# A graph layer's node update moved into the edge loop's buffers, with its inputs asked for in the last six groups and the last groups summed as small batches

## The chip, the cores and the metric

One core of one Trainium2 chip runs the kernel as one launch. The metric is the device time of that launch in microseconds (us); lower is better. The kernel before takes 4115.59 us (median of 3 runs, 4114.87 to 4116.8).

A core has five engines with a queue of instructions each: TensorE (PE; its weight loads are shown apart as PEld), VectorE (DVE), ScalarE (ACT), GpSimd (POOL) and SyncE (SP). [...] DMA transfers are started from a queue (SP's, ACT's or POOL's) and land later.

## The reference

A graph of 12,500 nodes with 64 features and 412,500 edges with 32 features, the edges sorted by receiver. Cut to what matters:

```python
h = relu(layernorm(x))
msg_in = concat(h[senders], h[receivers], edge)          # 412,500 x 160
messages = silu(msg_in @ W1 + b1) @ W2 + b2
logits = silu(msg_in @ Wa1 + ba1) @ Wa2 + ba2
att = softmax(logits, axis=0)                            # over all edges
agg = segment_sum(messages * att, receivers)             # per node
x = x + silu(concat(h, agg) @ Wu1 + bu1) @ Wu2 + bu2     # the node update
```

The softmax runs over all edges of the graph, so its maximum and its sum are known only at the end. The kernel keeps a running maximum and corrects what was summed under an older one.

## The kernel before, in words

**Head.** Nodes are normalised and two tables are written to DRAM: `ts_d` (sender's half of the first layer) and `tr_d` (receiver's half).

**Edge loop.** 403 groups (NG) of 1,024 edges each, as 8 tiles of 128 (K = 8). Each group `g` goes through these steps, which are functions in `one_pass`:

- `load(g)`: POOL starts eight indirect gathers of sender rows into a `gs` tile (L487; a ring of 8 `gs` tiles). Every eleventh group takes one of the eight tiles with row loads from SP in its place. SP loads the receivers' windows (`wins`, L506, three in turn) and, every fourth group, edge features `eo` and receivers' numbers `db` for four groups (two buffers of each in pool `work2`). DVE builds a selection in `eo` (L513), and PE multiplies it with the windows into the PSUM tile `pe` (L517; three tiles `pe` of two banks each).
- `begin(g)`: DVE adds `pe` and `gs` (L523), ACT takes the tanh (L526).
- `end(g)`: DVE makes the message (L536, kept in one of eight `acts` tiles) and the logits (L542, L544, L547). When `g` closes a batch, `top` reduces the batch's logits and transposes the maximum on PE (L557 to L564).
- `weigh(s)`: DVE takes the running maximum `nmax` from it (L571 to L574), ACT makes the factor `scale` for older sums (L575) and the weights `p` (L578). A new batch starts every 4 groups, and `starts` ends with the single groups 400, 401 and 402.
- `sum_up(g)`, which runs five groups late: `by_node` (DVE makes weighted selections, L588; PE sums edges to nodes into `sp`, L594), `out_of` (ACT copies `sp`, L600), `project` (PE, L605) and `put` (DVE adds the result to `sums` and notes the maximum in `stand`, L618 to L624). `put` works for one group two steps after its `by_node`.

`pin` keeps the order of the program among the instructions that it wraps; DMA starts are not pinned, and a scheduler places them in SP's queue. The PSUM tile `mt` exists once and is shared by the projection and the transposed maximum.

In groups 399 to 402 the loop drains: `upto` says how many further `sum_up` calls follow each `end`, and all of them are over when the loop ends.

**Node update** (L715 to L790). Thirteen tiles of 8 x 128 nodes, the last one of 2 x 128. Pools of its own are opened after the loop: `upd` in SBUF (three buffers of each name) and `upd_ps` in PSUM (`fac` twice, `th` twice, `po` three times). Per tile `t`:

- `sums_of`: SP loads `bu_in` from `bq_d` (L741) and `xb` from `xb_d` (L743), 256 KB each. Both were computed during the edge loop. ACT makes the correction `fac` = exp (L746), DVE scales `sums` with it and with the softmax's inverse (L750), POOL adds `bu_in` (L755).
- `silu`: ACT's tanh `th` (L759), then DVE (L760).
- `second`: four matmuls on PE into `po` (L767; the profile counts each fp32 matmul twice).
- `rest`: DVE adds `xb` (L773), SP writes two halves to the output (L775).

The loop over tiles is skewed:

```python
for t in range(NT + 2):
    if t < NT:
        sums_of(t)
    if 1 <= t <= NT:
        silu(t - 1)
        second(t - 1)
    if t >= 2:
        rest(t - 2)
```

Of the kernel before, what the change touches and what calls it, by code (L numbers as in the profile page):

```python
# [45 lines left out]
I32 = mybir.dt.int32  # L46
# [318 lines left out]
def one_pass(tc, n_edges, v):  # L365
# [11 lines left out]
    starts = list(range(0, NG - 3, B)) + [NG - 3, NG - 2, NG - 1]  # L377
# [5 lines left out]
    with ExitStack() as ctx:  # L383
# [7 lines left out]
        base_hi = keep.tile([1, NG + 1], I32, name="base_hi")  # L391
        nc.vector.tensor_scalar(base_lo[:, :NG], base_sb[:, :NG], float(NH), float(W),
# [10 lines left out]
        nc.vector.memset(start[:, 1:2], BIG)  # L403
        w2u = keep.tile([S1, 2, U], F32, name="w2u")
# [9 lines left out]
        with tc.tile_pool(name="work2", bufs=2) as work2, \  # L414
# [57 lines left out]
            def registers(g, engine, at, base=base_sb, top=NP - 1):  # L472
                n = min(NQ, NG - g)
                _, regs = nc.values_load_multi_w_load_instructions(
                    base[0:1, g:g + n], engines=[engine], min_val=0, max_val=top,
                    skip_runtime_bounds_check_because=WHY)
                for i in range(n):
                    at[g + i] = regs[i]

            def load(g):  # L480

                t = g * K
                if g % NQ == 0:
                    registers(g, ENG.SP, at_sp)
                gs = gss[g] = gather.tile([P, K, C], F32, name="gs")
                for j in range(K - (g in alone)):
                    nc.gpsimd.indirect_dma_start(  # L487
                        out=gs[:, j, :], out_offset=None, in_=ts_d[:, :],
                        in_offset=bass.IndirectOffsetOnAxis(ap=src_sb[:, t + j:t + j + 1], axis=0))
                if g % NQ == 0:  # L490
                    n = min(NQ, NG - g) * E2
                    eo = work2.tile([P, NQ, E2], F32, name="eo")
                    db = work2.tile([WR, NQ, E2], I32, name="db")
                    for i in range(g, min(g + NQ, NG)):
                        ees[i] = eo[:, i - g, :], db[:, i - g, :]
                    nc.sync.dma_start(eo.rearrange("p g e -> p (g e)")[WR:, :n],
                                      edge[:, g * E2:g * E2 + n])
                    for r in range(2):
                        nc.sync.dma_start(
                            db.rearrange("p g e -> p (g e)")[r * R:(r + 1) * R, :n],  # L500
                            bass.AP(tensor=dst_row.tensor, offset=dst_row[r:r + 1, g * E2:].offset,
                                    ap=[[0, R], [1, n]]))
                eo, db = ees.pop(g)
                win = wins[g % WINS]
                for r in range(2):
                    nc.sync.dma_start(win[r * R:(r + 1) * R, :, r, :],  # L506
                                      tr_w[bass.ds(at_sp[g], R), :, :])
                for q in range(len(QUEUES)):
                    if QUEUES[q][0] == ENG.SP:
                        rows(q, g)  # L510
                for h in range(2):
                    e = slice(h * E2 // 2, (h + 1) * E2 // 2)
                    pin(nc.vector.tensor_scalar(eo[:WR, e], db[:, e], bj[:, g, h:h + 1], None,  # L513
                                                op0=ALU.is_equal))
                pe = pes[g] = pre_ps.tile([P, K, C], F32, name="pe")
                for q in range(H):
                    pin(nc.tensor.matmul(pe[:, 2 * q:2 * q + 2, :], eo[:, q * P:(q + 1) * P],  # L517
                                         win[:, q // 2, :, :], start=True, stop=True))
# [9 lines left out]
            def end(g):  # L528
# [18 lines left out]
                pin(nc.vector.tensor_reduce(lgs[s][:, k:k + K], att, AX.X, ALU.add))  # L547
                if g == starts[s] + size[s] - 1:
                    mts[s] = top(s)
# [58 lines left out]
            def put(g):  # L608

                if g % NQ == 0:  # L610
# [3 lines left out]
                pp = pps.pop(g)  # L614
                for h, at in enumerate((at_lo, at_hi)):
                    rows, cols = slice(h * U, (h + 1) * U), bass.ds(at[g], W)
                    if g == starts[s]:
                        pin(nc.vector.scalar_tensor_tensor(sums[rows, cols], sums[rows, cols],  # L618
                                                           scale[rows, s:s + 1], pp[rows],
                                                           op0=ALU.mult, op1=ALU.add))  # L620
                    else:
                        pin(nc.vector.tensor_tensor(sums[rows, cols], sums[rows, cols], pp[rows],  # L622
                                                    ALU.add))
                    pin(nc.vector.tensor_copy(stand[rows, cols],  # L624
                                              nmax[rows, s + 1:s + 2].to_broadcast([U, W])))
# [4 lines left out]
            def weigh_upto(s):  # L630
                while weighed[0] <= s:
                    weigh(weighed[0])
                    weighed[0] += 1

            def sum_up(g):
# [11 lines left out]
                if g is not None:  # L647
                    s = batch[g]
                    weigh_upto(s)
                    if g == starts[s]:  # L650
                        pin(nc.vector.scalar_tensor_tensor(total, total, scale[:, s:s + 1],
                                                           psums.pop(s), op0=ALU.mult, op1=ALU.add))
# [7 lines left out]
            for g in range(NG):  # L660
                more = None
                if done <= g - B - 1 or g >= NG - 3 and done < g:
# [16 lines left out]
                if more:  # L679
                    next(more)  # L680
                end(g)
# [3 lines left out]
                if g >= NG - 4:  # L685
                    upto = g + (-3, -1, 0, 1)[g - NG + 4]
                    for i in list(range(done, upto)) + [None, None] * (g == NG - 1):
                        for _ in sum_up(i):
                            pass
                        if i == done and g < NG - 1:  # L690
                            weigh_upto(batch[g])
                    done = max(done, upto)
# [22 lines left out]

        with tc.tile_pool(name="upd1", bufs=1) as upd1, \
                tc.tile_pool(name="upd", bufs=3) as work, \
                tc.tile_pool(name="upd_ps", bufs=2, space=PSUM) as upd_ps:
            sv, fv = (t[:, W:W + NH].rearrange("f (p b) -> f p b", b=NB) for t in (sums, stand))
            last = nmax[:, NS:NS + 1]  # L720
            ones = upd1.tile([P, P], F32, name="ones")
            nc.vector.memset(ones, 1.0)
            all_ps = upd_ps.tile([P, P], F32, name="all_ps", bufs=1)
            nc.tensor.matmul(all_ps[:, 0:1], ones, total, start=True, stop=True)
            inv = upd1.tile([P, 1], F32, name="inv")
            nc.vector.reciprocal(inv, all_ps[:, 0:1])

            tc.mark_branch_hint_location("again", "LikelyTaken",
                                         engines=[ENG.SP, ENG.DVE, ENG.PE, ENG.Activation])
            assert NB % 2 == 0  # L730
            bs, xs, us, ths, pos = {}, {}, {}, {}, {}

            def width(t):
                return min(NC, NB - t * NC)

            def sums_of(t):

                n = width(t)
                cols = P // 2 * n
                bs[t] = work.tile([P, P // 2 * NC], F32, name="bu_in")[:, :cols]  # L740
                nc.sync.dma_start(bs[t], bq_d[t, :, :cols])  # L741
                xs[t] = work.tile([P, NC * D], F32, name="xb")[:, :n * D]
                nc.sync.dma_start(xs[t], xb_d[t, :, :n * D])  # L743
                at = slice(t * NC, t * NC + n)
                fac = upd_ps.tile([P, P // 2 * NC], F32, name="fac")[:, :cols]
                pin(nc.scalar.activation(fac.rearrange("u (p b) -> u p b", b=n), fv[:, :, at], AF.Exp,  # L746
                                         bias=last, scale=-1.0))
                us[t] = work.tile([P, P // 2 * NC], F32, name="uT")[:, :cols]
                for k in range(2):
                    pin(nc.vector.scalar_tensor_tensor(  # L750
                        us[t].rearrange("u (k p i) -> u k p i", k=2, i=n // 2)[:, k],
# [3 lines left out]
                pin(nc.gpsimd.tensor_tensor(us[t], us[t], bs.pop(t), ALU.add))  # L755

            def silu(t):
                th = upd_ps.tile([P, P // 2 * NC], F32, name="th")[:, :P // 2 * width(t)]
                pin(nc.scalar.activation(th, us[t], AF.Tanh, scale=0.5))  # L759
                pin(nc.vector.scalar_tensor_tensor(us[t], th, 1.0, us[t], op0=ALU.add, op1=ALU.mult))  # L760

            def second(t):
                n = width(t) // 2
                uv = us.pop(t).rearrange("u (m i) -> u i m", i=n)
                po = pos[t] = upd_ps.tile([P, H, 2, D], F32, name="po", bufs=3)[:, :n]
# [3 lines left out]
            def rest(t):  # L769
                n = width(t)  # L770
                res = work.tile([P, NC * D], F32, name="res")[:, :n * D]
# [6 lines left out]

            for t in range(NT + 2):
                if t < NT:  # L780
                    sums_of(t)
# [7 lines left out]
            for _ in range(3):  # L789
                pin(nc.vector.memset(work.tile([P, NC * D], F32, name="res")[:, 0:1], 0.0))  # L790
# [246 lines left out]
```

## Time and profile before

| what | value |
|---|---|
| median of 3 runs | 4115.59 us |
| the profiled execution's own time / its span | 4115.52 us / 4113.8 us |
| POOL busy (gathers almost alone) | 3035.8 us, 74% |
| DVE busy | 3021.4 us, 73% |
| PE busy / PEld busy | 2284.8 us / 1852.9 us |
| ACT busy | 584.3 us, 14% |
| last gather starts | 4042.24 us |
| DVE begins the last group (`begin(402)`) | 4050.81 us |
| DVE begins the node update (first L750) | 4066.28 us |
| last output's DVE step begins | 4107.0 us |
| DMA rate, 4066.3 to 4110 us | 216 GB/s |

A row of a timeline gives start, busy time, engine, line, operation, tiles, shape and count; in brackets stands how long the engine was idle before it, and what ended that. SPq is the time in which SP starts DMAs. A window's row gives the busy time of each engine in a stretch, with the clock that TensorE was granted, the busy share of the DMA engines and what they moved. The page's part on the chain that ended last is empty for this run, so the end is followed by hand in the timeline.

### The profile page before, as it was taken

What the parts mean: (1) busy time and instruction counts of PE and PEld (TensorE: products, weight loads), DVE (VectorE), ACT (ScalarE), POOL (GpSimd) and SP (SyncE); (2) the same over time, 40 slices, a digit from 0 to 9 for tenths busy, and PEclk for the clock granted to TensorE, in tenths of its full rate; (3) what the DMA queues carried; (4) which work ended last, traced back from release to release, by engine and by line L of the source; (5) the groups of instructions that cost most, each with busy time, mean ns of one, the idle gap of its engine ahead of it and who ended that gap; (6) DMA issues with size and microseconds to landing.
All of it is one profiled execution on the core that took longest, in us unless ns stands there. A gap on an engine that the chain in (4) does not pass through costs nothing.

```text
span 4113.8 us, 59789 instructions
## 1 busy us (share of the span) xinstructions
PE 2284.8 (56%) x10980; PEld 1852.9 (45%) x10980; DVE 3021.4 (73%) x8518; ACT 584.3 (14%) x1235; POOL 3035.8 (74%) x3213
## 2 busy tenths in 40 slices
PE   5555545555556555556555555555555555555555
PEld 4444434444445444444444444444444444444444
DVE  6777867777777777777777777777777777777777
ACT  3211111111111111111111111111111111111112
POOL 3777777777777777777777777777777777777773
PEclk8666666666565666665566666666666556566665
DMA  7344443443434333333333333333333333333334
GB/s 270 88 102 101 99 105 92 105 101 97 102 93 99 86 91 84 88 91 81 91 84 89 91 81 91 83 89 91 81 91 82 91 91 81 92 81 90 91 78 112
DMA packets 220602, 393.50 MB, mean 96 GB/s; under 512 B 77077, under 2 KB 146554, under 8 KB 207034
## 3 DMA queue, kind: packets, MB, share of 16 engines
q0 software_dynamic: 102016, 209.13, 20.8%
q1 hardware_dynamic: 116826, 170.81, 17.0%
q10 hardware_dynamic: 1376, 9.67, 0.6%
q14 instruction: 294, 2.41, 0.2%
q8 instruction: 90, 1.47, 0.2%
HBM read 363.58 MB, written 25.72 MB: 95 GB/s over the span
## 4 chain that ended last, share of the span: by engine, by line


## 5 line engine op out<-in xcount | busy, mean ns | idle before, releaser
L487 POOL DMA_INDIRECT gs<-ts_d,src_sb x3188 | 3018.7, 947 | 1022.1 <-issue 952.1
L517 PE MATMUL pe<-wins,eo 128*128 128x256 f32 x3224 | 1477.3, 638 | 967.7 <-DVE eo L513 819.6
L517 PEld LDWEIGHTS pe<-wins,eo 128*128 128x128 f32 x3224 | 1000.5, 325 | 1265.8 <-DVE eo L513 970.2
L523 DVE TENSOR_TENSOR gs<-pe,gs 128x1024 f32<-128x1024 f32 (+1 forms) x403 | 487.7, 1211 | 775.5 <-DMA gs<-ts_d,src_sb 740.0
L526 ACT ACTIVATE pe<-gs 128x1024 f32<-128x1024 f32 x403 | 413.8, 1027 | 2585.7 <-DVE gs L523 1997.7
L588 DVE TENSOR_SCALAR wt<-iota_w,dloc,p 128x40 f32<-128x40 f32 x3224 | 734.0, 320 | 0.1
L594 PE MATMUL sp<-wt,acts 128*65 128x40 f32 x6448 | 608.9, 267 | 0.7 <-DVE wt L588 0.7
L594 PEld LDWEIGHTS sp<-wt,acts 128*65 128x65 f32 x6448 | 578.7, 183 | 1.0 <-DVE wt L588 0.8
L605 PEld LDWEIGHTS mt<-ss,w2u 65*128 65x128 f32 x806 | 224.8, 293 | 371.3 <-issue 321.5
L513 DVE TENSOR_SCALAR eo<-db,bj 64x256 f32<-64x256 int32 x806 | 259.7, 360 | 158.6 <-DMA db<-in_dst_row_dram 151.5
L564 PE MATMUL mt<-ident,mx 128*128 128x128 f32 x103 | 45.1, 437 | 547.3 <-DVE sums L622 538.2
L605 PE MATMUL mt<-ss,w2u 65*128 65x40 f32 x806 | 184.9, 324 | 261.4 <-DVE gm L571 257.9
L542 DVE SCALAR_TENSOR_TENSOR pe<-pe,gs 128x512 f32<-128x512 f32 x403 | 281.3, 698 | 13.0
L544 DVE TENSOR_TENSOR pe<-pe,w_all 128x512 f32<-128x512 f32 x403 | 281.4, 698 | 12.8
L536 DVE SCALAR_TENSOR_TENSOR acts<-pe,gs 128x512 f32<-128x512 f32 x403 | 278.2, 690 | 15.7 <-ACT pe L526 4.0
L547 DVE TENSOR_REDUCE lg<-pe 128x8 f32<-128x512 f32 x403 | 278.4, 691 | 13.7
L564 PEld LDWEIGHTS mt<-ident,mx 128*128 128x128 f32 x103 | 18.4, 179 | 557.7 <-issue 556.0
L624 DVE COPY stand<-nmax 64x40 f32 x806 | 163.4, 203 | 0.6
L622 DVE TENSOR_TENSOR sums<-sums,mt 64x40 f32 x600 | 113.2, 189 | 15.0 <-PE mt L605 10.9
L575 ACT ACTIVATE scale<-fall 128x1 f32<-128x1 f32 x103 | 20.9, 203 | 645.1 <-DVE fall L574 629.2
L600 ACT COPY ss<-sp 65x40 f32<-65x40 f32 x403 | 73.5, 182 | 20.7 <-PE sp L594 20.3
L618 DVE SCALAR_TENSOR_TENSOR sums<-sums,scale,mt 64x40 f32 x206 | 51.6, 251 | 11.4 <-PE mt L605 7.3
(92 smaller groups left out, 577.7 us busy)
## 6 DMA issues: line engine op xcount, KB each, us to landing
one_gs<-ts_d SPq DMA_DIRECT2D x4608, 0.5 KB
eo<-in_edge_dram SPq DMA_DIRECT2D x100, 512.0 KB
db<-in_dst_row_dram SPq DMA_DIRECT2D x200, 256.0 KB
gs<-ts_d,src_sb POOLq DMA_INDIRECT x3188
wins<-tr_d SPq DMA_DIRECT2D x806, 32.0 KB
ts_d<-ts SPq DMA_DIRECT2D x5, 896.0 KB
tr_d<-tr ACTq DMA_DIRECT2D x5, 896.0 KB
hT_d<-hT ACTq DMA_DIRECT2D x1, 3136.0 KB
```

The lines of the kernel that those rows point to most:

```text
L487: nc.gpsimd.indirect_dma_start(out=gs[:, j, :], out_offset=None, in_=ts_d[:, :], in_offset=bass.IndirectOffsetOnAxis(ap=src_sb[:, t + j:t ...
L513: pin(nc.vector.tensor_scalar(eo[:WR, e], db[:, e], bj[:, g, h:h + 1], None, op0=ALU.is_equal))
L517: pin(nc.tensor.matmul(pe[:, 2 * q:2 * q + 2, :], eo[:, q * P:(q + 1) * P], win[:, q // 2, :, :], start=True, stop=True))
L523: pin(nc.vector.tensor_tensor(gss[g][:, :n, :], pes[g][:, :n, :], gss[g][:, :n, :], ALU.add))
L526: pin(nc.scalar.activation(pes[g], gss[g], AF.Tanh))
L536: pin(nc.vector.scalar_tensor_tensor(acts[g % ACTS][:, :, 0:U], th[:, :, U:C], 1.0, gs[:, :, U:C], op0=ALU.add, op1=ALU.mult))
L542: pin(nc.vector.scalar_tensor_tensor(att, th[:, :, 0:U], 1.0, gs[:, :, 0:U], op0=ALU.add, op1=ALU.mult))
L544: pin(nc.vector.tensor_tensor(att, att, wa2[:, None, :].to_broadcast([P, K, U]), ALU.mult))
L547: pin(nc.vector.tensor_reduce(lgs[s][:, k:k + K], att, AX.X, ALU.add))
L588: pin(nc.vector.tensor_scalar(wt[:, j, :], iota_w[:, j // H, :], dloc[:, g * K + j:g * K + j + 1], p[:, k + j:k + j + 1], op0=ALU.is_equal ...
L594: pin(nc.tensor.matmul(sp, acts[g % ACTS][:, j, :], wt[:, j, :], start=j == 0, stop=j == K - 1))
L605: pin(nc.tensor.matmul(pp, w2u.rearrange("s h u -> s (h u)"), sps.pop(g), start=True, stop=True))
```

## The change

Three things change; all of them lie in the last six groups, the node update, and set-up ahead of the loop.

- **Batches.** The last starts are 392, 396, 398, 399, 400, 401, 402: two batches more (105 in place of 103). The extra `sum_up` calls are made after groups 396 to 399, one each, and from group 397 on each group also has one of its own. Groups 400 and 401 have one each, and group 402's steps are written out by hand behind the loop.
- **Inputs.** `bu_in` and `xb` of all 13 tiles are loaded by `inputs(t)`, called after groups 398, 399 and 401, into `eo` and `db` buffers (tiles 0 to 7) and into five `gs` tiles (8 to 12). `eo` and `db` are moved for it from `work2` to two fixed buffers of each.
- **Update in the loop's buffers.** `ut` and `res` are the two halves of three `gs` tiles. `fac`, `th` and `po` share three `pe` tiles: `fac` and `th` in the first bank of a tile, `po` in the second. `fac` of tile t + 1 is now made before `th` of tile t - 1.

The rest of the diff: `base_lo` and `base_hi` are zeroed, `ones` and `inv` move to set-up, and the branch hint moves ahead of the last group. In `put`, the parts `sums` and `stand` can be called apart.

```diff
-    starts = list(range(0, NG - 3, B)) + [NG - 3, NG - 2, NG - 1]
+    starts = list(range(0, NG - 7, B)) + [NG - 7] + list(range(NG - 5, NG))
...
+        nc.vector.memset(base_lo, 0)
+        nc.vector.memset(base_hi, 0)
...
+        eos = [keep.tile([P, NQ, E2], F32, name=f"eo{i}") for i in range(2)]
+        dbs = [keep.tile([P, NQ, E2], F32, name=f"db{i}") for i in range(2)]
...
-                    eo = work2.tile([P, NQ, E2], F32, name="eo")
-                    db = work2.tile([WR, NQ, E2], I32, name="db")
+                    eo = eos[g // NQ % 2]
+                    db = dbs[g // NQ % 2][:WR].bitcast(I32)
...
+            def inputs(t):
+                n = P // 2 * NC
+                if t < 8:
+                    i = (t // 4 + (NG - 1) // NQ + 1) % 2
+                    bs[t], xs[t] = (b[i][:, t % 4, :n] for b in (eos, dbs))
+                else:
+                    gs = gather.tile([P, K, C], F32, name="gs").rearrange("p k c -> p (k c)")
+                    bs[t], xs[t] = gs[:, :n], gs[:, n:]
+                m = width(t)
+                bs[t], xs[t] = bs[t][:, :P // 2 * m], xs[t][:, :m * D]
+                nc.sync.dma_start(bs[t], bq_d[t, :, :P // 2 * m])
+                nc.sync.dma_start(xs[t], xb_d[t, :, :m * D])
...
-                if done <= g - B - 1 or g >= NG - 3 and done < g:
+                if done <= g - B - 1 or g >= NG - 6 and done < g:
                     more, done = sum_up(done), done + 1
...
-                if g >= NG - 4:
-                    upto = g + (-3, -1, 0, 1)[g - NG + 4]
-                    for i in list(range(done, upto)) + [None, None] * (g == NG - 1):
-                        for _ in sum_up(i):
-                            pass
-                        if i == done and g < NG - 1:
-                            weigh_upto(batch[g])
-                    done = max(done, upto)
+                if NG - 7 <= g < NG - 3:
+                    for _ in sum_up(done):
+                        pass
+                    done += 1
+                    if g == starts[batch[g]] + size[batch[g]] - 1:
+                        weigh_upto(batch[g])
+                for t in {NG - 5: [0, 1], NG - 4: [2, 3], NG - 2: range(4, NT)}.get(g, []):
+                    inputs(t)
...
+            two, one = at[1], at[0]
+            end(NG - 1, then=lambda: put(two))
+            out_of(one)
+            weigh_upto(NS - 1)
+            totals(NS - 1)
+            project(one)
+            by_node(NG - 1)
+            put(one, "stand")
+            put(NG - 1, "stand")
+            put(one, "sums")
+            last = nmax[:, NS:NS + 1]
+            free = [gather.tile([P, K, C], F32, name="gs").rearrange("p k c -> p (k c)") for _ in range(3)]
+            uts, outs = ([f[:, i * P // 2 * NC:(i + 1) * P // 2 * NC] for f in free] for i in range(2))
+            free_ps = [pre_ps.tile([P, K, C], F32, name="pe") for _ in range(3)]
...
+            def factor(t):
+                n = width(t)
+                fac = facs[t] = free_ps[t % 3].rearrange("p k c -> p (k c)")[:, :P // 2 * n]
...
             def silu(t):
+                n = P // 2 * width(t)
+                ut, th = uts[t % 3][:, :n], free_ps[t % 3].rearrange("p k c -> p (k c)")[:, :n]
...
             def second(t):
+                po = pos[t] = free_ps[t % 3][:, H:, :].rearrange("p i (h d) -> p i h d", h=2)[:, :n]
...
+            factor(0)
+            all_ps = one_ps.tile([P, 4, P], F32, name="mt")[:, 0, :]
+            pin(nc.tensor.matmul(all_ps[:, 0:1], ones, total, start=True, stop=True))
+            pin(nc.vector.reciprocal(inv, all_ps[:, 0:1]))
+            out_of(NG - 1)
+            project(NG - 1)
+            put(NG - 1, "sums")
             for t in range(NT + 2):
                 if t < NT:
-                    sums_of(t)
+                    first(t)
+                if t + 1 < NT:
+                    factor(t + 1)
                 if 1 <= t <= NT:
                     silu(t - 1)
                     second(t - 1)
```

`first(t)` is the DVE and POOL part of the old `sums_of`.

## The prediction, made before the changed kernel had run

> **What bounds the kernel now.** I read the page's totals first, then windows over the last 130 us, then the timeline there, then its waits.
>
> ```profile
> L487 POOL DMA_INDIRECT gs<-ts_d,src_sb x3188 | 3018.7, 947 | 1022.1 <-issue 952.1
> ```
>
> 947 ns of gather and 0.30 us of issue make 1.25 us; 3188 of them make 3977 us, the whole way from about 66 us to the last gather. POOL paces the loop at 9.98 us per group (8 gathers). A DVE group has 7.9 us of work (below), so nothing before group 396 sets the end, and the change leaves POOL's gathers alone. Only what follows the last gather counts, some 71 us.
>
> ```profile
> 4015.00:4026.00 11.00, 5.38 (x29) 4.41 (x29) 10.53 (x35) 1.33 (x3) 8.27 (x9) 0.66 0.23 55
> 4026.00:4040.00 14.00, 9.90 (x67) 8.77 (x67) 12.54 (x49) 2.51 (x10) 10.64 (x12) 0.62 0.21 52
> 4040.00:4051.00 11.00, 5.33 (x41) 4.80 (x40) 10.38 (x38) 1.70 (x6) 2.57 (x3) 0.50 0.13 25
> 4051.00:4066.30 15.30, 8.40 (x57) 7.37 (x56) 11.64 (x49) 3.34 (x11) 0.00 (x0) 0.50 0.06 12
> 4066.30:4082.00 15.70, 11.29 (x43) 10.30 (x43) 12.71 (x26) 7.43 (x13) 7.59 (x6) 0.59 0.80 249
> 4082.00:4107.30 25.30, 14.90 (x57) 13.35 (x56) 13.14 (x27) 6.55 (x12) 8.00 (x7) 0.58 0.72 209
> ```
>
> Columns: PE, PEld, DVE, ACT, POOL busy, TensorE clock, DMA share, GB/s. From group 399 (4015) DVE is full: 10.53 of 11.00, 12.54 of 14.00, 10.38 of 11.00. In the update it is full until 4082 (12.71 of 15.70) and then half idle (13.14 of 25.30), with DMA at 72 to 80%.
>
> ```profile
> 4042.24 0.94 POOL L487 DMA_INDIRECT gs<-ts_d,src_sb  x1 [0.30 <-issue]
> ...
> 4050.81 1.22 DVE L523 TENSOR_TENSOR gs<-pe,gs 128x1024 f32<-128x1024 f32 x1 [0.21 <-issue]
> ...
> 4066.28 1.66 DVE L750 SCALAR_TENSOR_TENSOR uT<-sums,inv,fac 128x256 f32<-128x256 f32 x4
> ```
>
> A group's DVE start follows its last gather's start by 2.83 us when it waits for it (gather at 4012.28, DVE at 4015.11). The last group could begin at 4045.07; it begins at 4050.81, because DVE is behind by 5.7 us. From there to the first L750 are 15.5 us, and from L750 to the span's end 47.5 us.
>
> ```profile
> POOL uT L755 <- DMA bu_in<-bq_d: 13.8, 5, 5.0
> ```
>
> In the update POOL waits 13.8 us for `bu_in` (plus part of a first wait). Undisturbed, L773 follows itself by 2.2 us (4072.53 to 4081.29 for four tiles), which is DVE's own work of 2.24 us per tile (0.86 + 0.69 + 0.69).
>
> **What a page says.** The Trainium skill, "PSUM — Partial Sum Buffer", sections Terms and Specifications, forbids two engines on one bank and quadrant at once, and lets engines work side by side in different banks. By that rule `fac`/`th` in one bank of a `pe` tile and `po` in the other need no wait on each other. The trace of before cannot show the case: there `fac`, `th` and `po` are tiles of their own, and `fac` follows `th` without a wait (4086.13, 4086.67 below). I go by the changed program as built. In it `fac` of tile t + 3 waits for the last matmul of tile t, the very count that L773's successor (`rest` of tile t) waits for. The two share a tile, and the program makes one wait for the other though their banks differ.
> For the loads beside the gathers, "DMA: Bandwidth & Descriptors", Queues, rings and completion order, says each DMA engine takes turns among the queues it has work for. So loads share with the gathers rather than block them; before, 55 GB/s run in these groups and 249 GB/s in the update, so there is room.
>
> **Part 1, the groups.** Work of DVE by start-to-start times: begin and put 1.89 (4005.13 to 4007.02), selection 0.53, eight weights 1.9, message and logits 2.95, closing a batch 0.4. An extra `sum_up` is put and weights, 2.6 (4022.77 to 4025.31); weighing is 0.9 up to the next begin (4025.34 to 4026.24). Group 399 of before, with one extra `sum_up`, one closing and one weighing, took 4015.11 to 4026.24 = 11.13 us. The changed order, from the same start 3984.99 of group 396:
> - 396 (extra sum, weighing): 10.8, ends 3995.8. 397 (all, and register loads, 0.3): 11.4, 4007.2. 398: 11.1, 4018.3. 399 (and a total): 11.6, 4029.9.
> - 400 (own sum, closing, total): 7.8, 4037.7. 401 (own sum, weighing with ACT's answer awaited, 0.55): 8.7, 4046.4.
>
> Gathers land ahead of each (3994.9, 4005.1, 4015.1, 4025.1, 4035.1, 4045.1), so DVE stays the limit. Two more batches cost 1.4 us each, inside these sums. begin(402) comes at 4046.4, **4.4 us earlier**. Bounds: 5.7 earlier (the gather), 0 if PE's chains stall DVE in the doubled groups.
> After begin(402) both programs have two weightings of eight (groups 401 and 402), the logits, a weighing and the last puts. The new one weighs 401 there too (0.7), but under the tanh that DVE awaited anyway, and its `stand` copies move ahead of the last projection; I keep 15.5 us. First L750 at 4061.9.
>
> **Part 2, the inputs.** 26 loads (6.4 MB) leave the update for about 3982 to 4036. In SP's new order the windows of group 401 stand behind nine of them and those of 402 behind fourteen. SP asks for windows some 20 us before use:
>
> ```profile
> 3982.31 19.34 SPq L506 DMA_DIRECT2D wins<-tr_d  x6
> ```
>
> Nine loads are 2.3 MB, 9 us at 249 GB/s; so they are hidden, and cost the remainder in PE's L517 if that cover went. 6.4 MB in 54 us is 119 GB/s above 55. What late gathers cost is bounded by 0 and about 1 us (DVE has 0.9 us of slack against the gather of 397, more later). I take 0. The 13.8 us of waits for `bu_in` go.
>
> **Part 3, the update.** What is late next? ACT's queue is in order. It now holds fac(t+3), th(t+1), fac(t+4), th(t+2), and fac(t+3) waits for PE's second(t). So th(t+1), silu(t+1) and second(t+1) come behind second(t): a ring through PE, ACT, DVE, PE. Its pieces:
>
> ```profile
> 4065.15 1.30 ACT L746 ACTIVATE fac<-stand,nmax 128x512 f32<-128x512 f32 x2 [1.57 <-DVE stand L624]
> ...
> 4086.13 0.60 ACT L759 ACTIVATE th<-uT 128x512 f32<-128x512 f32 x1 [5.09 <-POOL uT L755]
> 4086.67 0.67 ACT L746 ACTIVATE fac<-stand,nmax 128x512 f32<-128x512 f32 x1
> 4086.77 0.69 DVE L760 SCALAR_TENSOR_TENSOR uT<-th,uT 128x512 f32<-128x512 f32 x1 [4.01 <-ACT th L759]
> ...
> 4087.61 2.21 PE L767 MATMUL po<-w_all,uT 128*128 128x128 f32 x8 [4.14 <-DVE uT L760]
> ```
>
> fac to the next ACT instruction 0.63 (1.30 less one 0.67); th to L760 0.63 (4086.13 to 4086.77); L760 to the matmuls 0.84 (4086.77 to 4087.61); the matmuls 2.21, and 0.09 to ACT (as for L600: 4039.09 to 4039.18). Sum **4.40 us per tile against 2.24**. DVE (2.24) and POOL (1.27) fit beside it, so no engine is full.
> From the first L750: 0.98 to POOL, 1.30 to th, 0.63, 0.84, 2.25 = 6.0 to the end of second(0). Ten ring steps follow, as fac(12) is the last factor; its step is 4.1, for it is a 128-wide one: 43.7. Tiles 11 and 12 add 3.1 to the last L773. From there to the span's end as before, 4107.3 to 4113.8: 6.45. Together 59.25, against 47.5: **11.7 us later**.
>
> At no cost: the memsets of set-up lie beside the first gathers. The moved hint is one instruction on four engines, 0 to 0.5, taken 0. POOL's adds stay 13.
>
> **Sum.** Against the profiled span: 4113.8 - 4.4 + 11.75 = 4121.15, +7.35. Its own time, 4115.52, is 0.07 below the median, so 4115.59 + 7.35 = 4122.9. About 0.2% (8.2 us) is what a measurement of this kernel can tell from no change; the forecast is a loss just inside it.
>
> **The rivals.**
> - **The ring is not felt.** If the wait for second(t) were mostly met before ACT reaches it, the update runs at 2.2 us per tile: 6.0 + 11 x 2.2 + 0.9 + 6.45 = 37.55 behind 4061.9, so 4099.5 in the span, time **4101.2**. For it: loads gone, DVE free. Against: the wait is in the program, and L760 to second's end alone is 3.05 us. It decides as soon as the four pieces of the ring sum below 2.24 us; they sum to 4.40.
> - **No earlier start.** The doubled `sum_up` calls share the one `mt` tile with the batch maxima, at TensorE clock 0.50 to 0.66; each late projection stalls a put on DVE, and DVE in 397 to 401 has no slack. If begin(402) stays at 4050.8 the ring's cost stands alone: **4127.3**. It passes 0.2% once begin(402) is later than 4047.3. For it: before, DVE waited 0.83 us for L605 in group 400. Against: half of the extra work moves to groups where DVE had 2 to 3 us idle each.
> - **The inputs do no good.** If loads were late, L755 would wait again; at 4.4 us per tile there is twice the time for them, so the time is the forecast's.
>
> **Chances.** Forecast 0.73 (4119 to 4127), some two fifths of it beyond 0.2%; no earlier start, or worse, 0.17; ring not felt 0.10. The first and the nearer part of the second make the range: 4118 to 4129. Faster by over 0.2%: 0.10; within: 0.47; slower: 0.43.
>
> **What would show it.** ACT's `fac` (now into a `pe` tile) waiting for PE in the update, about 2 us on each of ten tiles; matmul groups 4.4 us apart; POOL never waiting for DMA; begin(402) near 4046.4; DMA rate in the update halved. I am wrong if matmul groups lie 2.2 us apart, or if begin(402) is outside 4045 to 4048.

## The result and the profile after

| | before | changed |
|---|---|---|
| median, beside each other on one chip (20 runs each) | 4114.48 us (4112.01 to 4117.64) | 4120.57 us (4119.0 to 4122.98) |
| ratio, with its 95% interval | | 1.0015 [1.0009, 1.0022] |
| span of the profiled execution | 4113.8 us | 4121.2 us |
| last gather starts | 4042.24 | 4041.59 |
| `begin(402)` on VectorE | 4050.81 | 4048.39 |
| first step of the node update | 4066.28 | 4064.10 |
| from there to the span's end | 47.5 us | 57.1 us |

The change costs 6.1 us, and the interval is clear of no change. The two profiled executions lie 7.4 us apart: the groups end 2.2 us earlier, and the node update takes 9.6 us more.

Each experiment below was timed beside the kernel before. In the last eight of the twelve runs every kernel took 6.2 to 6.4 ms, the one before included (medians 6232, 6253, 6383 and 6415 us), with GpSimd idle for 3084 us between gathers in one of them against 1020 us in the changed kernel and nearly all of it put down to no instruction; of those runs I read only the stretch from group 396 on, and no verdict rests on their times.

The windows of the changed kernel, cut at the same events as before's (columns: busy time of PE, PEld, DVE, ACT, POOL, then TensorE clock, DMA share, GB/s):

```profile
4015.00:4026.00 11.00, 7.14 (x36) 5.92 (x35) 9.14 (x36) 1.82 (x6) 8.26 (x10) 0.59 0.51 148
4026.00:4040.00 14.00, 9.07 (x62) 7.89 (x61) 13.05 (x44) 1.82 (x6) 10.65 (x12) 0.71 0.43 117
4040.00:4051.00 11.00, 3.49 (x20) 2.69 (x20) 8.90 (x29) 2.85 (x7) 1.92 (x3) 0.54 0.12 21
4051.00:4064.10 13.10, 6.82 (x41) 5.85 (x41) 10.22 (x45) 3.16 (x11) 0.00 (x0) 0.50 0.00 0
4064.10:4082.00 17.90, 8.05 (x30) 7.17 (x30) 9.33 (x19) 4.23 (x7) 6.28 (x5) 0.50 0.13 30
4082.00:4115.20 33.20, 18.83 (x70) 16.48 (x69) 16.55 (x33) 8.96 (x16) 9.31 (x8) 0.50 0.29 70
```

The loads have moved: 148 and 117 GB/s in the groups (55 and 52 before), 30 and 70 in the update (249 and 209 before). In the last two rows no engine is busy for much more than half of the time, and neither is the DMA: something waits in a circle. The timeline of two tiles of the update shows it:

```profile
4065.20 2.49 POOL L789 TENSOR_TENSOR gs<-gs,eo 128x512 f32<-128x512 f32 x2 [22.67 <-DVE gs L784]
...
4067.88 2.23 PE L802 MATMUL pe<-w_all,gs 128*128 128x128 f32 x8 [4.46 <-DVE gs L795]
...
4070.15 0.69 ACT L776 ACTIVATE pe<-stand,nmax 128x512 f32<-128x512 f32 x1 [3.05 <-PE pe L802]
4070.78 0.58 ACT L794 ACTIVATE pe<-gs 128x512 f32<-128x512 f32 x1
4071.39 0.69 DVE L795 SCALAR_TENSOR_TENSOR gs<-pe,gs 128x512 f32<-128x512 f32 x1 [2.79 <-ACT pe L794]
...
4072.14 2.23 PE L802 MATMUL pe<-w_all,gs 128*128 128x128 f32 x8 [2.02 <-DVE gs L795]
```

L789 is GpSimd's add, L776 the Exp that makes `fac`, L794 the Tanh `th`, L795 the silu, L802 the matmuls into `po`. The Exp starts when the matmuls end, the Tanh when the Exp is through, the silu behind it, and the next matmuls behind that: 4.26 us from one matmul group to the next. The waits of the stretch from 4064 us on count it (columns: us in all, times, longest):

```profile
ACT pe L776 <- PE pe L802: 30.5, 10, 3.1
```

Ten waits of 3.05 us. The Exp is for a tile three later than these matmuls, and nothing needs it yet; it is the Tanh behind it in ScalarE's queue that is late. GpSimd's two adds had made the input of that Tanh by 4067.69, and it ran at 4070.78.

### The profile page after: what moved, and what is told of

It is laid out like the page before. It is cut to its first block, busy times and chain, and to the rows that moved or that the text cites. A ratio compares the mean times of both kernels' runs of the same rounds, so it can differ in the third digit from the quotient of the medians.

```text
span 4121.2 us, 59835 instructions
## 1 busy us (share of the span) xinstructions
PE 2281.0 (55%) x10982; PEld 1847.0 (45%) x10982; DVE 3020.4 (73%) x8532; ACT 585.2 (14%) x1241; POOL 3037.6 (74%) x3213
## 3 DMA queue, kind: packets, MB, share of 16 engines
q1 hardware_dynamic: 116826, 170.81, 17.1%
```

## The experiments

**Theory.** The loss is this ring. `fac` of tile t + 3 lies in the first bank of the PSUM tile whose second bank takes `po` of tile t, the program makes the Exp wait for those matmuls, and the next Tanh stands behind it in ScalarE's queue. **Rivals.** The update is slow because it lives in the loop's buffers, or because loads and stores contend with it; or it is the order of the two ScalarE instructions alone, or PSUM alone. For the groups: the early loads make gathers late, against projections that stall VectorE.

**1. The Exp behind the Tanh.**

```diff
-                if t + 1 < NT:
-                    factor(t + 1)
                 if 1 <= t <= NT:
                     silu(t - 1)
                     second(t - 1)
+                if t + 1 < NT:
+                    factor(t + 1)
```

> The changed kernel, with one thing moved: in the update loop the Exp that makes fac of tile t+1 is issued behind the Tanh, the silu and the matmuls of tile t-1 instead of ahead of them; the tiles that fac, th and po share stay as they are. Theory of the ring (the Exp waits for the matmuls of the tile whose PSUM buffer it reuses, and the next tile's Tanh stands behind it on ScalarE): the wait of 3.05 us at the Exp no longer holds up a Tanh, matmul groups come 2.3 to 2.5 us apart instead of 4.26, ten steps give 18 to 20 us back, so 4101 us (4099 to 4105), about 14 below the kernel before. Rival, the update is slow because its inputs and results lie in the loop's buffers or because the loads and stores contend with it: the order on ScalarE changes nothing, 4120 us, groups 4.2 apart.

4104.9 us (4102.71 to 4106.56), ratio to before 0.9976 [0.9967, 0.9985]. The update takes 40.7 us instead of 57.1. Two matmul groups are merged in a row here (x16):

```profile
4071.84 4.40 PE L802 MATMUL pe<-w_all,gs 128*128 128x128 f32 x16 [1.13 <-DVE gs L795]
4076.96 4.40 PE L802 MATMUL pe<-w_all,gs 128*128 128x128 f32 x16 [0.72 <-DVE gs L795]
```

5.12 us for two tiles, 2.56 each. The loop's buffers, loads and stores are unchanged, so that rival falls. The shared tile is still felt: the Exp waits for PE ten times (9.6 us, but the Tanh behind it is late by only 0.8 us once and 0.2 us or less after that), and four times the add at L808, which reads `po`, waits for an Exp that writes the other bank (4.3 us).

**2. `fac` in a buffer of its own.**

```diff
-                fac = facs[t] = free_ps[t % 3].rearrange("p k c -> p (k c)")[:, :P // 2 * n]
+                fac = facs[t] = wins[t % 3].rearrange("p a b c -> p (a b c)")[:, :P // 2 * n]
```

> The changed kernel with its order on ScalarE kept, but fac written to three SBUF buffers of its own (the loop's window buffers, free by then) instead of the first bank of the PSUM tile that th and po use. Theory of the ring: the Exp has nothing to wait for but the multiply of three tiles earlier, the Tanh behind it is no longer late, 2.3 to 2.6 us a tile and 4101 us (4098 to 4106), the same as with the order changed. Rival, it is the order of the two ScalarE instructions (the Exp's own 0.63 us ahead of the Tanh) and not the buffer: at most 0.6 us a tile comes back, 4114 us. Rival, contention: 4120 us.

4099.24 us (4098.31 to 4100.4), ratio 0.9963 [0.995, 0.9977]: 15 us below the kernel before and 21 below the changed one (timed apart; before had 4114.44 and 4114.48 us), the lowest time measured. The order on ScalarE is the changed kernel's, so the order by itself is not the cause; it hurts only where the Exp has something to wait for. The update takes 37.05 us, and from the third tile on TensorE does not stop (82 of the 98 fp32 passes in one row):

```profile
4063.36 4.00 PE L802 MATMUL pe<-w_all,gs 128*128 128x128 f32 x16 [4.48 <-DVE gs L795]
4067.77 21.96 PE L802 MATMUL pe<-w_all,gs 128*128 128x128 f32 x82 [0.41 <-DVE gs L795]
```

I had expected the same as in 1. Of the 5.7 us between them the update accounts for 3.65 (40.7 against 37.05), which fits the waits on the shared tile that 1 kept. The rest arose ahead of the update, where the two programs are the same; its cause is not shown.

**3. The groups alone.** The changed kernel up to the end of the loop, without `inputs`, and behind it the update of before with its pools, word for word:

```diff
-                for t in {NG - 5: [0, 1], NG - 4: [2, 3], NG - 2: range(4, NT)}.get(g, []):
-                    inputs(t)
...
+        with tc.tile_pool(name="upd1", bufs=1) as upd1, \
+                tc.tile_pool(name="upd", bufs=3) as work, \
+                tc.tile_pool(name="upd_ps", bufs=2, space=PSUM) as upd_ps:
```

> The first part alone: the last groups' small batches and their sums one group behind as in the changed kernel, and behind them the node update of the kernel before, with its own pools and its loads at the time of use. Theory: the groups part is a gain and the update a loss. Without the early loads the gathers land as in the kernel before (2.9 us after their start, not 4.8), begin of the last group comes 4 us earlier than before (4046.4 to 4047) and the end with it: 4111 us (4109 to 4113), 3.5 below the kernel before. Rival, the groups part gains nothing by itself and its sums (0.5 us waits for projections) come back in the drain: 4114 to 4116 us.

4113.01 us (4111.11 to 4115.01), ratio 0.9997 [0.9989, 1.0005]: no difference from before that can be told. The groups do what was expected; the two rows (here L525 is `begin`) are those of groups 396 and 402, the last gather having started at 4040.86:

```profile
3983.55 1.09 DVE L525 TENSOR_TENSOR gs<-pe,gs 128x896 f32<-128x896 f32 x1 [0.86 <-DMA gs<-ts_d,src_sb]
...
4045.67 1.23 DVE L525 TENSOR_TENSOR gs<-pe,gs 128x1024 f32<-128x1024 f32 x1 [0.21 <-issue]
```

Counted from the last gather's start, which differs by up to 4 us between executions, `begin(402)` comes at 4.81 us, against 8.57 in the kernel before and 6.80 in the changed one. But from there to the update are 17.1 us here and 15.5 before, so 1.6 of the 3.8 us are given back: the weighing of group 401 now comes behind `begin(402)`, and from there to the last projection 14.7 us pass (4060.34) where before took 12.8 (4063.64). The changed kernel pays for this too, but issues the softmax's total ahead of the last projection and needs 15.7 us. The expected 3.5 us in the time did not come: by the medians it is 1.4 us, within the noise.

**4. The loads later.** On top of 1:

```diff
-                for t in {NG - 5: [0, 1], NG - 4: [2, 3], NG - 2: range(4, NT)}.get(g, []):
+                for t in {NG - 2: range(NT)}.get(g, []):
...
-                nc.sync.dma_start(bs[t], bq_d[t, :, :P // 2 * m])
-                nc.sync.dma_start(xs[t], xb_d[t, :, :m * D])
+                pin(nc.sync.dma_start(bs[t], bq_d[t, :, :P // 2 * m]))
+                pin(nc.sync.dma_start(xs[t], xb_d[t, :, :m * D]))
```

> The order of the first experiment, and the 26 input loads pinned on their queue behind the window loads of the last group instead of being spread over the last six groups, so that they start about 4005 to 4010 us into the span and not at 3981. Theory: the loads at 3981 to 3995 (228 GB/s) delay the gather of group 396 by 1.9 us, and VectorE carries that delay to the end; later loads give it back, group 396 begins near 3984.5, and the time is 1.5 to 2 us below that of the first experiment, 4099 us. The loads still come in time: at 180 GB/s the 6.3 MB take 35 us. Rival, the gather was late for another reason or the delay is absorbed further on: same time as the first experiment. Rival, the loads now come too late and GpSimd's adds wait for them: 1 to 5 us above it.

4104.65 us (4102.83 to 4106.0), the same as 1: a miss. Group 396 does begin with a shorter wait, but now the last group waits for its gather:

```profile
3981.64 1.09 DVE L530 TENSOR_TENSOR gs<-pe,gs 128x896 f32<-128x896 f32 x1 [0.94 <-DMA gs<-ts_d,src_sb]
...
4045.29 1.23 DVE L530 TENSOR_TENSOR gs<-pe,gs 128x1024 f32<-128x1024 f32 x1 [1.13 <-DMA gs<-ts_d,src_sb]
```

The five kernels beside before, on this point (the rate is that of all DMA between the two events of the third column):

| kernel | loads | from group 396's last gather to `begin(396)` | DMA there | `begin(402)` after the last gather's start |
|---|---|---|---|---|
| before | in the update | 2.91 us | 72 GB/s | 8.57 us |
| changed | from group 395 on | 4.81 | 289 | 6.80 |
| 1 | the same | 3.69 | 225 | 6.82 |
| 2 | the same | 3.30 | 170 | 5.56 |
| 3 | in the update | 2.67 | 73 | 4.81 |
| 4 | from about group 397 on | 2.75 | 70 | 6.49 |

Where loads run beside gathers, one gather or another is late and `begin(402)` comes 0.8 to 2.0 us later than without them. The more the DMA moved, the later the gather was usable. In the changed kernel the first load was issued 0.12 us ahead of that gather, in 1 and 2 0.43 and 0.90 us behind it. Moving the loads by two groups only chose another gather. Each row is one execution.

**5 and 6. The loads at their time of use,** without the ring (on top of 2) and with it (on top of the changed kernel). The first load goes to an `acts` tile that the loop's last matmuls read, the others follow pinned:

```diff
+            for t in range(3):
+                inputs(t)
             factor(0)
...
                 if t >= 2:
                     rest(t - 2)
+                    if t + 1 < NT:
+                        inputs(t + 1)
```

> fac in SBUF as in the second experiment (no ring), and the input loads put back to their time of use: the first behind the last matmuls of the loop, the others three tiles ahead, each pinned behind the stores of the tile three before. Theory (early loads are worth nothing behind the ring and much without it): GpSimd waits for the loads again as in the kernel before (8 to 10 waits, 16 to 20 us in all), the update takes 46 to 48 us instead of 37, and the time is 9 to 11 us above the second experiment: 4109 us (4107 to 4112). Rival, all of the update's gain over the kernel before comes from elsewhere (the loop's buffers, an earlier start): 4100 us.

> The changed kernel with its ring kept and only the input loads put back to their time of use. Theory: at 4.26 us a tile the ring leaves the DMA 768 KB a tile, 185 GB/s, under the 240 to 254 GB/s that the update of the third experiment drew, so the loads hide behind the ring and matmul groups stay 4.26 apart; the first tile's add waits 1 to 1.5 us for its load, and the gathers of the last groups are no longer disturbed (1 to 2 us): 4120 us (4118 to 4122), the same as the changed kernel. Rival, the early loads do help the changed kernel and the ring hides only a part: 4124 to 4130 us.

Times: 6247.0 us (before 6232.33; ratio 1.0026 [1.0011, 1.0041]) and 6256.01 us (1.0040 [1.0021, 1.0060]). What tells is the update. With the ring (6), the matmul groups keep their 4.26 us although six of GpSimd's thirteen adds wait for a load in the update; two rows:

```profile
6190.04 2.24 PE L802 MATMUL pe<-w_all,gs 128*128 128x128 f32 x8 [2.03 <-DVE gs L795]
6194.30 2.23 PE L802 MATMUL pe<-w_all,gs 128*128 128x128 f32 x8 [2.03 <-DVE gs L795]
```

Its update takes 59.2 us against 57.1, the 2 us coming with the last two tiles. So in the changed kernel the early loads are worth about 2 us in the update, if the DMA served both executions alike. Without the ring (5), GpSimd waits for loads again, and the matmuls with it:

```profile
6191.65 2.24 PE L802 MATMUL pe<-w_all,gs 128*128 128x128 f32 x8 [0.30 <-DVE gs L795]
6197.36 2.23 PE L802 MATMUL pe<-w_all,gs 128*128 128x128 f32 x8 [3.47 <-DVE gs L795]
```

55.4 us, against 37.05 in 2 and 37.2 in 7, which was timed on the same chip: here the early loads are worth 18 us. I had expected 46 to 48; whether the larger number is due to the pinned order or to the DMA's rate there (178 GB/s over 49.6 us, where 3 drew 225 over 41.2) stays open, but the sign and the order of size do not.

**7. No load beside a gather.** On top of 2, with all loads pinned behind one whose buffer was meant to be that of group 401:

```diff
+                if g == NG - 2:
+                    free = [gather.tile([P, K, C], F32, name="gs") for _ in range(2)]
+                    hold = [gather.tile([P, K, C], F32, name="gs") for _ in range(5)]
+                    for t in [NT - 1, *range(NT - 1)]:
+                        inputs(t)
```

> The second experiment, with all loads pinned behind one whose buffer is that of the group before the last, so that none starts before that group is done with it (about 4042 us into the span, behind the last gather). Theory: any load that runs while gathers still run makes a gather late on which VectorE then waits; with none, group 396 waits 0.9 us as in the third experiment instead of 1.5 to 3.0, and the last group begins 4.8 us behind the start of the last gather instead of 5.6 to 6.8: 1 to 2 us below the second experiment, 4098 us (4097 to 4099.5). The loads have 17 us to the first multiply and 37 us more. Rival, VectorE's own work sets the last groups and the gather wait is absorbed: same as the second experiment within 0.7 us. Rival, loads come late: GpSimd waits for DMA in the update, 4101 us or more.

6243.23 us (ratio 1.0011 [0.9986, 1.0035]). The update is as short as in 2, 37.2 us. It does not test the theory, for two reasons: the first load starts at 6141.01, while group 397 is worked on, so the buffer was not group 401's; and the last gather had started at 6123.22, when group 396 was just beginning, so no gather could be late in any case. What loads kept clear of all gathers would give is open.

**8, run four times (8, 11, 12, 13). Projections first.** On top of 7, in groups 396 to 399:

```diff
+                early = NG - 7 <= g < NG - 3
+                if more and early:
+                    next(more)
                 if g + AHEAD < NG:
                     load(g + AHEAD)
-                if more:
+                if more and not early:
                     next(more)
```

> The seventh, and in groups 396 to 399 the projection and the weighed sums of the group behind are issued ahead of the next group's window matmuls on TensorE instead of behind them. Theory: VectorE's waits of 1.3 and 1.5 us for a projection in groups 397 and 399 come from the window matmuls (3.8 us) ahead of it in TensorE's queue; they fall away and the last group begins 1.5 to 2.5 us earlier, as far as the last gather allows: 4096 us (4095 to 4097.5). Rival, the window matmuls of the next group are then late and VectorE waits at begin instead: same as the seventh or up to 2 us slower.

> The kernel of the eighth again (fac in SBUF, loads behind the last gathers, projections ahead of the window matmuls), for a time beside the kernel before on a chip where that takes its 4114 us. Theory: VectorE's waits for projections in groups 397 and 399 go and no load runs beside a gather: 4096 us (4095 to 4098), 18 below the kernel before and 24 below the changed kernel. Rival, the gathers set the pace of the last groups anyhow: 4099 us as in the second experiment.

> The kernel of the eighth once more, by itself (fac in SBUF, loads behind the last gathers, projections ahead of the window matmuls), for a time beside the kernel before where that takes its 4114 us. Theory: no load runs beside a gather and VectorE does not wait for projections in groups 397 and 399, so the last group begins 1 to 2 us earlier than in the second experiment: 4097 us (4095.5 to 4098.5). Rival, the gathers set the pace of the last groups anyhow, or the window matmuls are late in place of the projections: 4099 us or more, as in the second experiment.

> The kernel of the eighth a last time, for its time where the kernel before takes 4114 us. Theory: the update alone gives 20 us (37 us instead of 57), and without loads beside gathers and with one of the two projection waits gone the groups give 1 to 2 us more than in the second experiment: 4097.5 us (4096 to 4099). Rival, the groups give nothing more: 4099 us or above.

6220.14, 6382.23, 6243.83 and 6412.11 us; ratios 0.9985 [0.997, 1.0], 1.0001 [0.9978, 1.0024], 0.9982 [0.996, 1.0005] and 0.9998 [0.9981, 1.0015]. From `begin(396)` to `begin(402)` the four took 60.5, 62.2, 60.1 and 61.8 us, kernel 7 61.4. But in three of the four VectorE stood for 1.0 to 1.9 us in group 396 with no instruction named as the cause, and in kernel 7 for 0.34. From `begin(397)` on they took 48.8, 49.6, 49.5 and 49.2 us, kernel 7 50.35: a gain of 0.8 to 1.6 us. The rows say where: of kernel 7 the waits of `put` in groups 397 and 399, of kernel 8 the wait left in group 397 and the put of group 399, which waits no more:

```profile
6140.12 0.25 DVE L628 SCALAR_TENSOR_TENSOR sums<-sums,scale,mt 64x40 f32 x1 [1.48 <-PE mt L614]
6162.15 0.25 DVE L628 SCALAR_TENSOR_TENSOR sums<-sums,scale,mt 64x40 f32 x1 [0.95 <-PE mt L614]
```

```profile
6104.60 0.19 DVE L632 TENSOR_TENSOR sums<-sums,mt 64x40 f32 x1 [0.97 <-PE mt L614]
6129.13 0.24 DVE L628 SCALAR_TENSOR_TENSOR sums<-sums,scale,mt 64x40 f32 x1
```

The wait in group 399 went, and that group took 10.28 or 10.29 us in all four against 11.34. The one in group 397 stayed, for another put (0.97 to 1.79 us), and that group took 0.5 us less to 0.3 us more. The update took 36.9 to 37.4 us in all four. Why the ratios show so little of the 20 us that it saves stays open; the kernel before has no trace there. What the gain in the groups is worth at 4114 us is open too.

**9. Another bank.**

```diff
-                fac = facs[t] = free_ps[t % 3].rearrange("p k c -> p (k c)")[:, :P // 2 * n]
+                fac = facs[t] = free_ps[(t - 1) % 3].rearrange("p k c -> p (k c)")[:, P // 2 * NC:][:, :P // 2 * n]
```

> The changed kernel with its order and its PSUM tiles kept; only where fac of tile t+1 lies is changed: the second bank of the tile before (which po of tile t fills later) instead of the first bank of the tile whose matmuls are in flight. Theory of the ring: the Exp then waits for the stored result of one tile earlier, the chain spans two tiles instead of one (matmuls 2.2, add 0.7, Exp 0.65, Tanh 0.6, silu 0.7 us: 4.9 us for two), matmul groups come near 2.5 us apart and the time is 4103 us (4100 to 4106). Rival, fac in PSUM itself is what is slow, and only its move to SBUF or behind the Tanh helps: 4.2 us apart, 4120 us.

6398.73 us (before 6383.35; ratio 1.0033 [1.0014, 1.0051]). The update takes 43.2 us, with order, PSUM and sharing kept:

```profile
6356.62 2.23 PE L802 MATMUL pe<-w_all,gs 128*128 128x128 f32 x8 [0.78 <-DVE gs L795]
6359.44 2.23 PE L802 MATMUL pe<-w_all,gs 128*128 128x128 f32 x8 [0.59 <-DVE gs L795]
```

2.82 us a tile. The Exp now waits for L808 ("1.55 <-DVE gs L808" at 6354.38), which reads `po` of four tiles before; in the changed kernel it waited for the matmuls of three tiles before. PSUM as such is not slow; what counts is whose end the Exp waits for.

## Why the prediction was right, and where it was not

The time came within the range, 2.3 us below the forecast (1.1 of them because the kernel before read 1.1 us lower as well), and the mechanism is the one it named. That the span agrees, 4121.15 us against 4121.2, is luck, though: two errors of 2.2 us cancel, and they are worth more than the agreement.

- **The ring (part 3): right.** 4.40 us per tile were forecast, 4.26 measured; the ten steps took 42.3 us for 43.7, the tail 6.0 us for 6.45. The Exp's wait is 3.05 us rather than "about 2". That figure did not follow from the forecast's own pieces: 4.40 less the Exp's 0.63 and the Tanh's 0.60 is 3.2. Experiments 1, 2 and 9 each break the ring in another way and bring the update to 40.7, 37.05 and 43.2 us, so the cause is shown. The update in all: 57.1 us, forecast 59.25.
- **The page and the program.** The Trainium skill, "PSUM — Partial Sum Buffer", Specifications, lets ScalarE and VectorE work side by side in different banks, and its section Terms counts a collision with TensorE's writes only within one bank and quadrant; the forecast went by the program's wait in spite of it. The trace agrees with both: the 3.05 us are no collision in the memory, but a semaphore that the program set for the whole tile.
- **begin(402) (part 1): too optimistic.** Forecast 4046.4, measured 4048.39, just outside the 4045 to 4048 that I had named. Most of it is the step "I take 0" for late gathers (bounded by 0 and 1 us). Group 396 in the kernel before, then in the changed one, where the last row belongs to group 397:

```profile
3982.08 0.94 POOL L487 DMA_INDIRECT gs<-ts_d,src_sb  x1 [0.30 <-issue]
3984.99 1.09 DVE L523 TENSOR_TENSOR gs<-pe,gs 128x896 f32<-128x896 f32 x1 [1.10 <-DMA gs<-ts_d,src_sb]
```

```profile
3981.62 0.94 POOL L494 DMA_INDIRECT gs<-ts_d,src_sb  x1 [0.30 <-issue]
...
3986.43 1.09 DVE L530 TENSOR_TENSOR gs<-pe,gs 128x896 f32<-128x896 f32 x1 [3.00 <-DMA gs<-ts_d,src_sb]
...
4003.31 0.25 DVE L628 SCALAR_TENSOR_TENSOR sums<-sums,scale,mt 64x40 f32 x1 [1.30 <-PE mt L614]
```

  VectorE began 4.81 us after the last gather's start, against 2.91 before. That gather had no slack, since VectorE was waiting for it already; the slack that I quoted was that of group 397. So group 396 began 1.44 us later than the 3984.99 from which the forecast counts. From there to `begin(402)` it took 61.96 us, forecast 61.4. These 0.56 us, in groups 397 and 399, where puts waited 1.30 and 1.49 us for projections, are the partial form of the rival "no earlier start"; without the loads (3) the same stretch took 62.1 us.
- **The inputs (part 2): right, and as idle as the third rival said.** GpSimd never waits for a load in the update. The DMA rate fell further than "halved", to 30 and 70 GB/s from 249 and 209: 6.4 of the 9.6 MB had left a stretch that grew longer. Behind the ring the early loads are worth 2 us (6), about what they cost at the gathers (0.8 to 2.0). Without the ring they are worth 18 us (5 against 2).
- **"The ring is not felt", 4101.2 us:** not what happened, but a good forecast of the kernel without it (4099.24 and 4104.9 us; for the update 37.55 us, and 2 took 37.05).

So the change built the buffers and the loads for an update of 37 us, and one shared PSUM tile kept it at 57.

## What to carry to other kernels

When small buffers are packed into a larger tile, list for each writer whose last access to that *tile* it will wait for, and then what stands behind it in its queue: a wait for something that is needed much later costs nothing by itself, and all of it when the next urgent instruction is queued behind. If all engines and the DMA are half idle, add up one round of the waits; where the sum is the period, break one edge (a buffer, the order, another bank) before anything else is judged. A transfer moved to quiet time still meets the transfers there, so look for the one that is awaited without slack.

## What the runs showed of the hardware

- In every kernel with `fac` in SBUF (2, 5, 7 and the four runs of 8) the four multiplies of the first two tiles took 2.67 or 2.68 us; with `fac` in PSUM (changed, 1, 4, 6 and 9) 1.65 or 1.66. Of 2, then of 1:

```profile
4059.55 2.68 DVE L784 SCALAR_TENSOR_TENSOR gs<-sums,inv,wins 128x256 f32<-128x256 f32 x4
4060.66 1.29 POOL L789 TENSOR_TENSOR gs<-gs,eo 128x512 f32<-128x512 f32 x1 [21.43 <-DVE gs L784]
```

```profile
4062.93 1.66 DVE L784 SCALAR_TENSOR_TENSOR gs<-sums,inv,pe 128x256 f32<-128x256 f32 x4
```

  The longest of the 26 in experiment 2 took 1484 ns, the median 476; in 1 the longest took 480. It ran while GpSimd added two SBUF tiles, and in 1 GpSimd's add ran beside the fourth multiply too. That agrees with the Trainium skill, "SBUF — State Buffer", section "SBUF: two separate sides": a VectorE operation with two SBUF inputs and a GpSimd operation that reads SBUF exclude each other for the whole instruction. In 2 it cost 1 us once, since in later tiles the two hardly met (0.87 to 1.08 us for a pair). In 5, where the adds came late, four pairs took 1.48 to 1.89 us.
- With 256 KB loads from SP's queue under way, an indirect gather from GpSimd's queue was usable 3.30 to 4.81 us after its start, at 170 to 289 GB/s, against 2.67 to 2.91 us at 70 to 73 GB/s (one gather each of six kernels).
- TensorE was granted a clock of 0.50 through the changed update, where its matmuls came in short groups, and of 0.84 from 4067.77 to 4089.73 in experiment 2, where they ran end to end. The groups took 2.23 and 2.14 us, so the clock explains little of the difference between the kernels. What sets the clock these runs do not show.
